# Macaron block, attention beside precomputed units: the odd chunk's scores and keys and the next values issued ahead of the q and k correction, and the router's choice cut in two

## The chip, the core and the metric

The kernel runs on one core of a Trainium2 chip. A core has a matrix engine (TensorE, PE in the profile, with PEld for its weight loads), a vector engine (VectorE, DVE), an engine for activation functions and copies (ScalarE, ACT), a general engine (GpSimd, POOL) and an engine that mostly issues transfers (SyncE, SP). Every engine works off its own queue in order and waits for the others by semaphores. Matrix products land in PSUM, a small memory of eight banks, from which VectorE or ScalarE must read them. The metric is the device time of one execution in microseconds, the median of several runs; lower is better.

## The reference, cut to what matters

```python
x = x + 0.5 * ffn(layernorm(x))      # x: 8 sequences of 1024 tokens, 512 wide, fp32
x = x + attn(layernorm(x))
x = x + 0.5 * ffn(layernorm(x))

def attn(x):                         # 16 heads of 32
    q, k, v = exp(heads(x @ Wq.T + bq)), exp(heads(x @ Wk.T + bk)), heads(x @ Wv.T + bv)
    kv, k1 = cumsum(k[..., :, None] * v[..., None, :], 1), cumsum(k, 1)
    out = einsum("zsD,zsDd->zsd", q, kv) / sum(q * k1, -1, keepdims=True)
    return unheads(out) @ Wo.T + bo

def ffn(x):                          # 32 experts; each expert chooses 8 tokens of a sequence
    probs = softmax(x @ gate_w.T + gate_b, axis=tokens)
    vals, idx = top_k(probs over tokens, 8)
    merged = sum of the 8 chosen tokens weighted by vals
    o = gelu([merged, 1] @ w1) ; o = [o, 1] @ w2
    return scatter_add(o * vals at idx)
```

The attention is linear and causal: the running sums over tokens are formed chunk by chunk, with an exact causal product inside a chunk of 128 tokens.

## The kernel before, in words

The program runs in three stages. The first FFN's router reads all eight sequences. The first FFN then streams the expert weights from HBM, and beside it `speculate` (from line 1101) already projects q, k and v of the *input* for sequences 4 to 7 and keeps the products in HBM (`ahead_d`). Attention follows (`attention`, from line 950). Last is the second FFN, again a stream of weights. Its first weights are loaded during the last sequence of attention.

Attention goes through the eight sequences b, and in each through eight chunks c of 128 tokens. Two chunks make a unit u. While a unit is attended, the next one is projected by a generator, `ahead`, which the loop advances with `next(ahead)`; each `yield` in the generator is a place where the loop goes on with something else. Up to sequence 3 the units come from `project`, which computes q, k and v in full. From sequence 4 on (in the code `rest` is true, from chunk 6 of sequence 3 to chunk 5 of sequence 7, 16 units) they come from `project_rest` (line 623). That one loads the product made beside the first FFN (tile `pre`, by `load_ahead`), scales it by the token's reciprocal deviation, and adds a correction: what the first FFN added to a token is its row of choice weights (`pm`, spread over four partition groups as `pm4`, scaled as `pmr`) times the experts' outputs already turned through Wq, Wk and Wv (`oW`, `oWv`).

Its steps are: 1. on SP, for a sequence's first unit, four loads of `pm4`, and the load of the next unit's `pre`; on POOL the bias `bo` onto `xt`, `pmr` (L651) and the two products of `pre` (L655); on PE the spread of the deviations (`ps_rs`, L641). 2. the correction of q and k: PE `ps_qk` (L667), VectorE's two additions (L676), ScalarE's eight exponentials (L679). 3. the values: PE `ps_v` (L687) and VectorE `va` (L697). 4. the running sums of the keys on VectorE (L720), and q times these sums on POOL (`qk`, L731).

For a chunk, `scores` (L777) multiplies keys with queries for all 16 heads; VectorE masks half of the result (L788), ScalarE copies the other half (L793), POOL masks that (L795). `turn_keys` (L827, copy L829) turns the keys. `attend` multiplies masked scores with values (L841) and queries with the running key-value sum (L853), divides by the denominators (L862) and adds to the running sum (L873, copy L882). `denominators` (L739, reciprocal L747) and `spread_denominators` (L758, copies L765) serve a unit. `project_out` (L891, addition L898, statistics L314 and L315) belongs to the chunk before. The generator `begun` scatters the first FFN's outputs into the next sequence (L293, L300, addition L308, statistics) over chunks 2 to 5; the generator `gate`, from `route`, runs the second FFN's router for the sequence before, a step per chunk: deviations, logits, the choice of eight tokens (`choose`, lines 404 to 428), then `ps_pmT` (L523), `ps_m` (L543) and `ps_mT` (L566).

Two things limit the order. The PSUM tiles `sp0` and `sp1` exist once: the scores, the spread denominators and the q and k correction take turns in them. Other products share three banks, `mm`. And what is written is not quite what is issued: a planner goes through the program, simulates the engines with costs of its own, and gives each engine, whenever it is free there, the ready instruction that stands first in the program. So a later instruction can run ahead of an earlier one that waits.

Of the kernel before, what the change touches and what calls it, by code (L numbers as in the profile page):

```python
# [8 lines left out]
F32 = mybir.dt.float32  # L9
AF = mybir.ActivationFunctionType  # L10
ALU = mybir.AluOpType
# [4 lines left out]
P = 128  # L16
# [4 lines left out]
def kernel(  # L21
# [52 lines left out]
    nc = tc.nc  # L74
    B, S, D = x_in.shape
# [328 lines left out]
    def choose(t, lg, rows, g, name, listed=False, el=None):  # L404


        top = t.p2.tile([P, 8], F32, tag="top", name=f"top_{name}")
        nc.vector.max(top[rows, :], lg[rows, :])
        pinned = el is not None
        sm = t.p2.tile([P, 3], F32, tag="sm", name=f"sm_{name}")  # L410
        nc.vector.tensor_scalar_mul(sm[rows, 0:1], top[rows, 0:1], -1.0)
        rest = pm[:, g, :]
        nc.vector.match_replace(rest[rows, :], top[rows, :], lg[rows, :], -1.0e30)
        if listed and not pinned:
            nc.vector.max_index(chosen_idx[rows, g, :], top[rows, :], lg[rows, :])
        el = el if pinned else lg
# [6 lines left out]
        if pinned:  # L423
            tc.keep_in_program_order(kept)
        nc.vector.reciprocal(sm[rows, 2:3], sm[rows, 1:2])
        if pinned:
            return rest, sm[rows, 2:3], top
        return rest, sm[rows, 2:3]
# [51 lines left out]
    def route(t, s, b, el=None):  # L480
# [28 lines left out]
        chosen, r, *top = choose(t, lg, rows, g, f"b{b}", True, el)  # L509
# [113 lines left out]
    def project_rest(t, s, b, u):  # L623
# [4 lines left out]
        if u == 0:  # L628

            pm4 = s["pm4"] = t.s1.tile([P, S], F32, tag="pm4", name=f"pm4_{b}")  # L630
            r0 = 32 * (b % 4)
            for j in range(4):
                nc.sync.dma_start(pm4[E * j : E * (j + 1), :], pm[r0 : r0 + E, b // 4, :])
# [25 lines left out]

        qkT = open_unit(t, s, b, u)  # L660
# [22 lines left out]

        ps = [t.mm.tile([P, D], F32, tag="mm", name=f"ps_v_{b}_{u * U + i}") for i in range(U)]
        for i in range(U):
            r = slice(E * ((b + i) % 4), E * ((b + i) % 4 + 1))
            nc.tensor.matmul(  # L687
                ps[i],
                lhsT=pmr[r, i * P : (i + 1) * P],
                rhs=s["oWv", i][r, :],  # L690
                start=True,
                stop=True,
            )
        for i in range(U):
            c = u * U + i
            va = t.a2.tile([P, D], F32, tag="va", bufs=3, name=f"va_{b}_{c}")
            nc.vector.scalar_tensor_tensor(  # L697
                va,
                pre[:, (2 * NDC + i * 2) * UT : (2 * NDC + i * 2 + 2) * UT],
                rs[:, c : c + 1],  # L700
                ps[i],
                ALU.mult,
                ALU.add,
            )
            s["va", b, c] = va
        yield
        sum_keys(t, s, b, u)
        times_keys(t, s, b, u)
        yield

# [239 lines left out]
    def attention(t, early, preload):  # L950
# [47 lines left out]
        for b in range(B):  # L998
            for c in range(NCH):
# [23 lines left out]
                if b == B - 1 and c == NCH - 2:  # L1023
# [6 lines left out]
                    )  # L1030
                    gate = route(t, s, b, el)
                if rest and c % U:
                    turn_keys(t, s, b, c)
                    next(ahead)
                    next(gate, None)
                scores(t, s, b, c)
                if c % U == 0:
                    denominators(t, s, b, c // U)
                    if (nb, nu) == (NB0, 0):
# [9 lines left out]
                        )  # L1049
                        load_ahead(t, s, nb, nu)  # L1050
# [33 lines left out]
                if not (rest and c % U):  # L1084
                    next(gate, None)
# [3 lines left out]
                if rest and c % U == 0:  # L1089
                    next(ahead)  # L1090
# [578 lines left out]
```

## Time and profile before

| | us |
|---|---|
| median of 3 runs | 2604.81 (2599.36 to 2604.91) |
| the profiled execution's own time | 2606.22 |
| its span, first to last instruction | 2604.5 |
| attention, first to last `ps_o` | 887.5 to 1940.1 |
| PE busy | 2190.8 (84%) |
| DVE, ACT, POOL busy | 862.3, 500.4, 376.6 |
| PE `ps_o` L891, 512 instructions | 258.5 |
| mean granted TensorE clock | 0.915 |

The page gives each engine's busy time. A busy PE can still run at half clock: the granted clock stands in a row of its own. Instructions are named by engine, line and tiles (what is written, an arrow, what is read), and idle time by what ended it. fp32 matrix products are issued as two instructions each, so a `scores` of 16 products appears as 32. The two FFNs are the stretches in which the DMA engines are full; attention is the stretch between, in which they are mostly idle.

### The profile page before, as it was taken

The page shows a single profiled execution, that of the slowest core. Times are in us where ns is not written, and L with a number is a line of the kernel's source. Part 1 is how long each engine was busy: PE and PEld are TensorE (multiplying, and loading weights), DVE is VectorE, ACT ScalarE, POOL GpSimd, SP SyncE. Part 2 cuts the span into 40 slices and gives each one's busy share as a digit, 9 for nine tenths or more (in the row PEclk, how much of TensorE's full clock was granted, in tenths as well). Part 3 has the DMA queues.
Part 4 walks back from the last instruction along what each step waited for, and adds up shares of the span by engine and source line. Part 5 has one row for each costly group of instructions (what it writes and reads, how often), then busy time and mean ns, then how long its engine had stood idle before and what let it go on. Part 6 is the DMA issues. An engine that isn't in the chain of part 4 may idle for free.

```text
span 2604.5 us, 41783 instructions
## 1 busy us (share of the span) xinstructions
PE 2190.8 (84%) x18679; PEld 1153.6 (44%) x18679; DVE 862.3 (33%) x1495; ACT 500.4 (19%) x965; POOL 376.6 (14%) x345
## 2 busy tenths in 40 slices
PE   8799999898986999999999989999986565555555
PEld 5354545444533666666666655555551111101111
DVE  6411111111102443444534466777750000100002
ACT  6310000000000322222223243343430000000000
POOL 0000000000000212111122145545324000000002
PEclk9999999999998999999999989989888878777788
DMA  7799999999996000010100233333159999999995
GB/s 276 305 426 427 427 427 427 426 427 428 427 429 255 1 18 1 21 50 20 52 9 19 79 110 124 106 113 109 68 210 389 425 427 428 428 428 428 428 427 239
DMA packets 95635, 668.22 MB, mean 257 GB/s; under 512 B 18254, under 2 KB 22606, under 8 KB 58592
## 3 DMA queue, kind: packets, MB, share of 16 engines
q1 hardware_dynamic: 73952, 621.71, 58.1%
q10 hardware_dynamic: 18432, 35.66, 3.5%
q0 software_dynamic: 3072, 8.19, 0.8%
q8 instruction: 146, 2.39, 0.4%
q14 instruction: 33, 0.27, 0.0%
HBM read 614.34 MB, written 48.23 MB: 254 GB/s over the span
## 4 chain that ended last, share of the span: by engine, by line
PE 50%; issue 23%; DMA 16%; DVE 5%; ACT 2%; POOL 1%; SPq 0%; POOLq 0%; ACTq 0%; DVEq 0%
DMA w<-in_w 11%; PE ps_o L891 8%; PE ps_k L603 4%; PE ps_q L603 4%; PE ps_v L811 4%; PE ps_sk L1143 3%; PE ps_sq L1143 3%; PE p_ps L1256 3%; PE h_ps L1233 3%; PE ps_n L841 2%; PE sp L777 2%; PE ps_n L853 2%; PE ps_sv L1160 2%; DMA xg<-out,chosen_idx 2%; PE ps_sc L293 1%
## 5 line engine op out<-in xcount | busy, mean ns | idle before, releaser
L1233 PE MATMUL h_ps<-w,mT 128*8 128x512 f32 x2048 | 294.4, 703 | 126.2 <-DMA w<-in_w 124.3
L1242 DVE STREAM_TRANSPOSE hs<-h_ps 128x512 f32<-128x512 f32 x64 | 45.9, 717 | 721.6 <-PE h_ps L1233 716.3
L1256 PE MATMUL p_ps<-w,pm 128*32 128x512 f32 x1024 | 168.9, 790 | 130.3 <-DMA w<-in_w 122.0
L891 PE MATMUL ps_o<-wo_sb,at 128*128 128x512 f32 x512 | 258.5, 652 | 0.2
L1233 PEld LDWEIGHTS h_ps<-w,mT 128*8 128x8 f32 x2048 | 51.2, 95 | 342.4 <-issue 208.7
L1256 PE MATMUL p_ps<-w,gl 128*32 128x512 f32 x1024 | 133.5, 654 | 38.6 <-DMA w<-in_w 38.3
L594 POOL TENSOR_TENSOR xt<-xt,bo_sb 128x512 f32<-128x512 f32 x32 | 45.8, 1447 | 763.1 <-PE ps_ocT L338 703.4
L1256 PEld LDWEIGHTS p_ps<-w,pm 128*32 128x32 f32 x1024 | 36.0, 127 | 265.7 <-issue 136.5
L891 PEld LDWEIGHTS ps_o<-wo_sb,at 128*128 128x128 f32 x512 | 102.0, 210 | 115.0 <-issue 110.0
L795 POOL TENSOR_SCALAR_AFFINE_SELECT am<-am 128x512 f32<-128x512 f32 x128 | 79.0, 642 | 398.7 <-ACT am L793 260.8
L314 DVE BATCH_NORM_STATS2 st<-xt 128x6 f32<-128x512 f32 x192 | 128.4, 684 | 5.1 <-DMA xt<-in_x 2.5
L603 PE MATMUL ps_k<-xnT,wk_sb 128*128 128x256 f32 x512 | 115.3, 383 | 10.8 <-ACT xnT L339 10.8
L1249 ACT ACTIVATE pm<-a 128x128 f32<-128x128 f32 x32 | 9.9, 309 | 586.5 <-DVE a L1244 580.5
L1143 PE MATMUL ps_sq<-xcT,wq_sb 128*128 128x256 f32 x512 | 118.7, 388 | 4.1 <-ACT xcT L241 4.1
L1143 PE MATMUL ps_sk<-xcT,wk_sb 128*128 128x256 f32 x512 | 117.4, 385 | 0.0
L1160 PE MATMUL ps_sv<-wv_sb,xcT 128*128 128x512 f32 x256 | 115.6, 599 | 0.0
L811 PE MATMUL ps_v<-wv_sb,xnT 128*128 128x512 f32 x256 | 115.1, 593 | 0.0
L603 PE MATMUL ps_q<-xnT,wq_sb 128*128 128x256 f32 x512 | 115.1, 382 | 0.0
L1143 PEld LDWEIGHTS ps_sq<-xcT,wq_sb 128*128 128x128 f32 x512 | 96.8, 193 | 35.3 <-issue 17.4
L1143 PEld LDWEIGHTS ps_sk<-xcT,wk_sb 128*128 128x128 f32 x512 | 96.8, 192 | 27.6 <-issue 15.0
L603 PEld LDWEIGHTS ps_k<-xnT,wk_sb 128*128 128x128 f32 x512 | 95.8, 190 | 28.6 <-ACT xnT L339 14.7
L777 PE MATMUL sp<-un 32*128 32x128 f32 x2048 | 104.8, 302 | 3.9 <-DVE un L676 3.8
(246 smaller groups left out, 2846.3 us busy)
## 6 DMA issues: line engine op xcount, KB each, us to landing
w<-in_w SPq DMA_DIRECT2D x256, 2048.0 KB, 29.8
xt<-in_x SPq DMA_DIRECT2D x31, 1024.0 KB, 10.8
pre<-ahead_d SPq DMA_DIRECT2D x16, 1536.0 KB, 6.5
ahead_d<-ahead_qk ACTq DMA_DIRECT2D x16, 1024.0 KB, 11.5
out<-xt SPq DMA_DIRECT2D x16, 1024.0 KB, 5.4
xs<-in_x ACTq DMA_DIRECT2D x16, 512.0 KB, 19.7
ahead_d<-ahead_v ACTq DMA_DIRECT2D x16, 512.0 KB, 11.0
pm<-pm SPq DMA_DIRECT2D x16, 128.0 KB, 2.5
```

What stands on the lines that cost most here:

```text
L314: nc.vector.bn_stats(st, xt[:, c, :])
L603: nc.tensor.matmul(ps[:, o, :], lhsT=w_sb[n][:, dc, oc * P : (oc + 1) * P], rhs=xnT[:, dc, :], start=(dc == 0), stop=(dc == NDC - 1),)
L777: nc.tensor.matmul(sp[r // 2][:, r % 2, og, :], lhsT=kT[hr, og, cols], rhs=qT[hr, og, cols], start=True, stop=True,)
L795: nc.gpsimd.affine_select(out=am[1][:, i, :, :], in_=am[1][:, i, :, :], pattern=[[0, NDC], [1, P]], compare_op=ALU.is_ge, fill=0.0, base=0 ...
L811: nc.tensor.matmul(ps, lhsT=s["xnT", b, c // U][:, dc, cols], rhs=w_sb["v"][:, dc, :], start=(dc == 0), stop=(dc == NDC - 1),)
L841: nc.tensor.matmul(ps[hr, og, :], lhsT=va[:, (og * HG + r) * HD : (og * HG + r + 1) * HD], rhs=am[r // 2][:, r % 2, og, :], start=(og == 0 ...
L853: nc.tensor.matmul(ps[hr, og, :], lhsT=kv[hr, og, :], rhs=qT[hr, og, cols], start=False, stop=True, skip_group_check=True,)
L891: nc.tensor.matmul(ps, lhsT=at[:, oc, :], rhs=w_sb["o"][:, oc, :], start=(oc == 0), stop=(oc == NDC - 1),)
L1143: nc.tensor.matmul(ps[:, o, :], lhsT=w_sb[w][:, dc, oc * P : (oc + 1) * P], rhs=xcT[:, dc, :], start=(dc == 0), stop=(dc == NDC - 1),)
L1160: nc.tensor.matmul(ps, lhsT=xcT[:, dc, i * P : (i + 1) * P], rhs=w_sb["v"][:, dc, :], start=(dc == 0), stop=(dc == NDC - 1),)
L1233: nc.tensor.matmul(h[32 * j : 32 * j + B, :], lhsT=mT[:, dc, e, :], rhs=w1h[dc // 2][:, dc % 2, j * 512 : (j + 1) * 512], start=(dc == 0), ...
L1256: nc.tensor.matmul(pp[32 * j : 32 * (j + 1), :], lhsT=gl4[e % 4][:, q, :, :].rearrange("p i b -> p (i b)"), rhs=w2h[q // (NU // 2)][:, q % ...
```

## The change

Four edits, all in attention and its router.

1. In `project_rest` the values (step 3) come ahead of the correction of q and k (step 2), and the loads of `pm4` move into a function of their own, `load_rows`, which the loop calls before the generator is made; for sequence 4 that is also ahead of the load of its first `pre` and of `oWv`.
2. In the loop, for an even chunk with `rest`, `turn_keys` and `denominators` come after step 1 of the next unit instead of, for the denominators, directly behind the scores. After `attend` of the even chunk the odd chunk's scores and keys are issued, then the next unit's values, then its correction. Before, the correction stood directly behind `attend`, and the odd chunk's keys, the values and the odd chunk's scores behind it.
3. For an odd chunk with `rest` the scores, the keys and one `next(ahead)` are gone from its start; what is left is `project_out`, the scatter step, the key sums, the router's step and `attend`. The router's step stands just ahead of `attend` in every chunk now; before, it stood ahead of the odd chunk's scores.
4. The choice becomes a generator, `choosing`: maximum, negated maximum and indices, a `yield`, and then the replacement, the exponential and the rest. The router of a sequence so takes seven steps and not six. What is left of sequence 6's router is run through before the last sequence's own begins.

```diff
     def choose(t, lg, rows, g, name, listed=False, el=None):
+        *_, made = choosing(t, lg, rows, g, name, listed, el)
+        return made
+    def choosing(t, lg, rows, g, name, listed, el=None):
...
+        in_place = el is None
+        if listed and in_place:
+            nc.vector.max_index(chosen_idx[rows, g, :], top[rows, :], lg[rows, :])
+            yield None
         nc.vector.match_replace(rest[rows, :], top[rows, :], lg[rows, :], -1.0e30)
-        if listed and not pinned:
-            nc.vector.max_index(chosen_idx[rows, g, :], top[rows, :], lg[rows, :])
...
-        chosen, r, *top = choose(t, lg, rows, g, f"b{b}", True, el)
+        for made in choosing(t, lg, rows, g, f"b{b}", True, el):
+            if made is None:
+                yield
+        chosen, r, *top = made
...
+    def load_rows(t, s, b):
+        pm4 = s["pm4"] = t.s1.tile([P, S], F32, tag="pm4", name=f"pm4_{b}")
+        r0 = 32 * (b % 4)
+        for j in range(4):
+            nc.sync.dma_start(pm4[E * j : E * (j + 1), :], pm[r0 : r0 + E, b // 4, :])
...
+                    for _ in gate:
+                        pass
                     gate = route(t, s, b, el)
-                if rest and c % U:
-                    turn_keys(t, s, b, c)
-                    next(ahead)
-                    next(gate, None)
-                scores(t, s, b, c)
+                if not (rest and c % U):
+                    scores(t, s, b, c)
                 if c % U == 0:
-                    denominators(t, s, b, c // U)
+                    if not rest:
+                        denominators(t, s, b, c // U)
...
+                        load_rows(t, s, nb)
                         load_ahead(t, s, nb, nu)
...
+                    if (nb > NB0 and nu == 0) and rest:
+                        load_rows(t, s, nb)
                     if (nb, nu) > (0, 1):
                         of = project_rest if rest else project
                         ahead = of(t, s, nb, nu) if nb < B else iter(())
                         next(ahead, None)
+                    if rest:
+                        turn_keys(t, s, b, c)
+                        denominators(t, s, b, c // U)
...
-                if not (rest and c % U):
+                if not rest:
                     turn_keys(t, s, b, c)
...
-                if not (rest and c % U):
-                    next(gate, None)
+                next(gate, None)
                 attend(t, s, b, c)
                 if rest and c % U == 0:
+                    scores(t, s, b, c + 1)
+                    turn_keys(t, s, b, c + 1)
+                    next(ahead)
                     next(ahead)
```

More of the change, by code (lines that the diff above doesn't have):

```diff
@@ L404, in choose @@
     def choose(t, lg, rows, g, name, listed=False, el=None):
+        *_, made = choosing(t, lg, rows, g, name, listed, el)
+        return made
+    def choosing(t, lg, rows, g, name, listed, el=None):
         top = t.p2.tile([P, 8], F32, tag="top", name=f"top_{name}")
         nc.vector.max(top[rows, :], lg[rows, :])
-        pinned = el is not None
         sm = t.p2.tile([P, 3], F32, tag="sm", name=f"sm_{name}")
@@ L412, in choose @@
         rest = pm[:, g, :]
+        in_place = el is None
+        if listed and in_place:
+            nc.vector.max_index(chosen_idx[rows, g, :], top[rows, :], lg[rows, :])
+            yield None
         nc.vector.match_replace(rest[rows, :], top[rows, :], lg[rows, :], -1.0e30)
-        if listed and not pinned:
-            nc.vector.max_index(chosen_idx[rows, g, :], top[rows, :], lg[rows, :])
-        el = el if pinned else lg
+        el = lg if in_place else el
         nc.scalar.activation(
@@ L422, in choose @@
         )
-        if pinned:
+        if not in_place:
             tc.keep_in_program_order(kept)
         nc.vector.reciprocal(sm[rows, 2:3], sm[rows, 1:2])
-        if pinned:
-            return rest, sm[rows, 2:3], top
-        return rest, sm[rows, 2:3]
+        yield (rest, sm[rows, 2:3]) if in_place else (rest, sm[rows, 2:3], top)
     def gather_four(t, xs, rs4, chosen, r, g):
@@ L627, in project_rest @@
         pre = s.pop(("pre", b, u))
[L628 to L633, printed above, removed]
         for i in range(U):
@@ L658, in project_rest @@
         yield
+        ps = [t.mm.tile([P, D], F32, tag="mm", name=f"ps_v_{b}_{u * U + i}") for i in range(U)]
+        for i in range(U):
+            r = slice(E * ((b + i) % 4), E * ((b + i) % 4 + 1))
+            nc.tensor.matmul(
+                ps[i],
+                lhsT=pmr[r, i * P : (i + 1) * P],
+                rhs=s["oWv", i][r, :],
+                start=True,
+                stop=True,
+            )
+        for i in range(U):
+            c = u * U + i
+            va = t.a2.tile([P, D], F32, tag="va", bufs=3, name=f"va_{b}_{c}")
+            nc.vector.scalar_tensor_tensor(
+                va,
+                pre[:, (2 * NDC + i * 2) * UT : (2 * NDC + i * 2 + 2) * UT],
+                rs[:, c : c + 1],
+                ps[i],
+                ALU.mult,
+                ALU.add,
+            )
+            s["va", b, c] = va
+        yield
         qkT = open_unit(t, s, b, u)
@@ L682, in project_rest @@
         yield
[L684 to L706, printed above, removed]
         sum_keys(t, s, b, u)
```

## The prediction, made before the changed kernel ran

> **What bounds the kernel now.** I read the page's slices first, then stretches of the attention part, then windows of 3.41 us, then one unit instruction by instruction. The edit lies in attention, where it works with units projected beside the first FFN: sixteen corrections, from 1504 us to about 1904 us. The first four lines are four stretches of about a batch each (microseconds; busy time per engine; granted TensorE clock), with 15 corrections between them; the last line is the stretch before, with the first correction.
>
> ```profile
> core 0: us, PE busy (x) PEld busy (x) DVE busy (x) ACT busy (x) POOL busy (x), PEclk, DMA share, GB/s
> 1517.00:1624.00 107.00, 99.69 (x1403) 59.19 (x1395) 78.37 (x122) 41.96 (x80) 51.34 (x42) 0.92 0.31 107
> 1624.00:1730.00 106.00, 99.35 (x1357) 59.72 (x1357) 77.23 (x120) 41.75 (x80) 50.30 (x40) 0.90 0.31 108
> 1730.00:1836.00 106.00, 98.65 (x1377) 58.05 (x1377) 78.19 (x121) 41.97 (x80) 50.31 (x40) 0.92 0.31 108
> 1836.00:1940.00 104.00, 98.76 (x1360) 59.47 (x1354) 64.75 (x98) 43.24 (x83) 32.72 (x28) 0.92 0.32 116
> ...
> 1464.00:1517.00 53.00, 45.98 (x420) 28.03 (x422) 21.07 (x32) 12.64 (x24) 16.24 (x13) 0.87 0.39 129
> ```
>
> TensorE sets the pace, but not at full speed. Its idle time in the four stretches is 7.3+6.7+7.4+5.2 = 26.6 us. The clock is 1.0 or 0.5 at any moment, so a mean of 0.92 over 107 us is 17 us at half speed; the four sum to 17+21+17+17 = 72 us, which costs 36 us. So 62.6 us is lost over 15 units, 4.2 us each. The first unit's stretch loses 7.0 us idle and 6.9 us to the clock.
>
> The next lines are single windows of the same view, chosen on the grid on which the clock changes.
>
> ```profile
> 1602.27:1605.68 3.41, 2.81 (x16) 1.65 (x13) 2.89 (x3) 2.33 (x5) 2.91 (x5) 1.00 0.00 0
> 1636.40:1639.81 3.41, 2.11 (x41) 1.52 (x37) 3.27 (x6) 2.93 (x8) 0.00 (x0) 1.00 0.02 7
> 1639.81:1643.23 3.42, 3.42 (x5) 1.46 (x5) 3.42 (x5) 3.34 (x8) 0.84 (x1) 0.50 0.86 313
> 1660.29:1663.70 3.41, 2.11 (x15) 1.10 (x11) 3.15 (x4) 1.89 (x5) 0.84 (x1) 1.00 0.00 0
> 1663.70:1667.12 3.42, 3.42 (x29) 3.42 (x32) 1.18 (x2) 1.88 (x5) 0.00 (x0) 0.50 0.54 151
> ```
>
> A window in which PE is busy 62% (2.11 of 3.41 us) is followed by one or two at half clock; one busy 82% is not. So a gap of some 1.3 us in one window costs itself and then 1.7 or 3.4 us more.
>
> Where the gap lies, a timeline of one unit shows (start, duration, engine, line, in brackets the idle time before and who ended it):
>
> ```profile
> 1716.96 1.15 PE L667 MATMUL ps_qk<-pmr,oW 32*128 32x256 f32 x16
> 1717.94 1.02 PE L687 MATMUL ps_v<-oWv,pmr 32*128 32x512 f32 x4
> 1718.19 2.36 DVE L676 TENSOR_TENSOR un<-ps_qk,pre 128x1024 f32<-128x1024 f32 x2 [0.73 <-PE ps_qk L667]
> 1719.47 0.49 PE L777 MATMUL sp<-un 32*128 32x128 f32 x4 [0.51 <-DVE un L676]
> 1720.46 1.40 DVE L697 SCALAR_TENSOR_TENSOR va<-pre,rs,ps_v 128x512 f32<-128x512 f32 x2
> 1720.60 1.16 PE L777 MATMUL sp<-un 32*128 32x128 f32 x28 [0.64 <-DVE un L676]
> 1721.69 5.40 PE L891 MATMUL ps_o<-wo_sb,at 128*128 128x512 f32 x8
> 1721.78 2.43 DVE L720 TENSOR_TENSOR_SCAN un<-ones,un 128x256 f32<-128x256 f32 x4
> 1724.38 2.36 POOL L731 TENSOR_TENSOR qk<-un 128x1024 f32<-128x1024 f32 x1 [8.05 <-DVE un L720]
> ```
>
> The odd chunk's scores (L777) need the PSUM tiles that the correction (L667) has just filled, and wait until VectorE has added them (L676). Then `ps_o` runs its first half at half clock: 5.40 us, against 3.44 us at full clock. In this unit the gaps are 0.51 and 0.64 us; in the three others of the batch it is one gap of 1.3 us. That is 1.25 us x 15 = 19 us, and every half-clock window of the four stretches follows such a gap: 19 + 36 = 55 us hang on this place.
>
> **The change part by part.** *The new order on TensorE.* From the start of an even chunk's `ps_n` (t = 0): attend 2.4 us (1714.55 to 1716.96), the odd chunk's scores 1.1, its keys 0.6, the next values 1.0, so the correction begins at 5.1. It needs the score tiles emptied: VectorE's masked product (1.20, from 3.6) ends at 4.8, ScalarE's copy (1.0) at 4.6. No wait remains. Nothing else is queued on PE behind a new wait here. Removed: 55 us.
>
> *What comes late next.* On VectorE the two `va` (1.40) now precede the two additions (2.36): these begin at 6.6, not 0.1 us after the correction. The exponentials end 4.9 us after the additions begin, as in the timeline, at 11.5. The next even chunk's scores stand on PE after the correction (to 6.1), `ps_o` (3.44) and attend (2.4): at 12.0, 0.5 us of cover. The key sums end at 11.2 (4.6 us after the additions begin), POOL's `qk` at 13.7; the denominators, moved behind the scores, the spread of rs and the keys (1.1+0.6+0.6), come at 14.3: 0.6 us of cover. The reciprocal (1.74) ends at 16.8, its reader `ps_rr` comes behind another 3.44 us of `ps_o` at 18.3. So a plain unit has no wait, with thin cover.
>
> In seven units VectorE has more: two scatter additions and two statistics (2 x 0.67 + 2 x 0.69 + 0.34 = 3.1 us a chunk, six units) or the choice. If that goes ahead of the key sums, against 1.05 us of PE work that comes with it, the denominators wait up to 3.1 - 1.05 - 0.6 = 1.4 us; if it goes behind, nothing. I take 1.0 us, nearer the full wait because VectorE is 73% busy already, and with it one window at half clock, 1.7 us. Given back: 7 x 2.7 = 19 us; bounds 0 and, as the slower rival prices it, 85.
>
> *The first unit.* PE waits 6.6 us there for `pmr` (1497.9 to 1504.5) and then runs at half clock. The four `pm4` loads now go ahead of `pre` and `oWv` on SP's queue (their issue takes 2.95 us). They can land 2.5 us after issue (page, part 6) or 9 us (as now): 1496 to 1502.5; `pre` moves from 1498.6 to 1501.5, its first product (2.3) to 1503.8. The odd chunk's scores fill 1.1 us of the wait. `ps_o`, now at 1511.1, starts at some 1505: 6 us gained; bounds 0 and 9. In later batches these loads keep their place on SP's queue, where `pre` is issued over 20 us ahead of use; its slot is now freed by the additions instead of `va`, 1 us later in the unit: nothing, and at most 1 us a unit without that cover.
>
> *The choice in two steps.* MAX8, FIND_INDEX8 and MATCH_REPLACE8 (1.2 us each) stay; the index now precedes the replacement, and what follows comes one chunk later, `ps_mT` (1.9 us on PE) in chunk 6 instead of 5. Work is moved, none added. Later: POOL and SP see one transfer, the next `xt` load behind `ps_m`, one chunk (13 us) later; the load of 10.8 us is used some 60 us on. Batches 1 to 3 have it too: there VectorE is under half busy (278 of 604 us, 860 to 1464 us), so nothing; bounds -3 and +4 us. For the last batch the leftover step is run ahead of the final router: 0, at most 1.9 us.
>
> *After attention.* The second FFN streams weights (DMA share 0.96 from 1940 us on) and starts where attention ends, so the gain passes through whole.
>
> Sum: 55 - 19 + 6 = 42 us. The profiled execution took 2606.2 us (span 2604.5), 1.4 us over the median of the runs: 2606.2 - 42 - 1.4 = 2563 us.
>
> **A rule against a row.** The rows give the half-clock windows to gaps of 1.3 us. The Trainium skill's page "TensorE: Matmul & The Clock Gate" (section "HAM oscillation — how this bites in real kernels") says that the clock drops over idle gaps longer than about 3.4 us, a whole window. By that, these gaps would not halve the clock and closing them would not give it back. The windows above contradict it: 38% idle is enough here.
>
> **The rivals.** *Nothing comes late:* 55 + 6 = 61 us, 2544. For it: every cover computed is positive. Against: 0.5 and 0.6 us of it.
>
> *Each unit gets a wait:* project_out's addition and statistics (0.69+0.69+0.18) ahead of the key sums take the 0.6 us and 1.0 more, with the half-clock window 2.7 us in all 15: 55 - 40 + 6 = 21 us, 2584.
>
> *Slower: the key sums in the written order.* They are written behind project_out and the scatter on VectorE. Held to that, they start at 11.2 (after `ps_o` at 9.5 and 1.6 us), `qk` ends at 16.1 and the denominators wait 1.8 us, with scatter 3.8; each with 1.7 to 3.4 us of half clock: 8 x 4.35 + 7 x 7.2 = 85 us against 61, so 2629. It decides from 4.1 us a unit on. For it: the written order. Against: the shown unit, where the sums (1721.78) ran ahead of the masked product written before them (1724.12), so the planner pulls ready work forward.
>
> *The half clock is not due to the gap* and stays: 19 idle + 6 - 7 = 18 us, 2587. This is where the page's rule would lead. *The change does not do it:* the planner issues much the same order: 2605.
>
> **How the numbers follow.** Chances: the forecast 0.36, nothing late 0.24, a wait in each unit 0.18, clock unrelated 0.04, no effect 0.04, slower 0.14. Faster by over 0.2% (5.2 us, about what a measurement tells from no change): 0.82; within: 0.04; slower: 0.14. The range leaves out the last two cases: up to 2600. Down to 2534, 10 us under "nothing late", since all the loss counted in the five stretches is 76 us (2528).
>
> **What would show it.** Right: no wait of the odd scores on L676's additions; the correction behind `ps_v`; four stretches near 96 us at a clock of 0.96 or more; `ps_o` at 3.4 to 3.7 us. Wrong: `ps_den` waiting for POOL `qk`, the even scores for ScalarE's exponentials, or a clock still near 0.92.

## The result, and the profile after

The changed kernel takes 2569.12 us (median of 4 runs, 2568.23 to 2570.43), the kernel before beside it 2602.09 us (2598.60 to 2604.91): a ratio of 0.9869, 95% interval 0.9849 to 0.9889. The forecast was 2563 us. So the gain is 33.0 us by the medians. The profiled execution took 2568.23 us, its span is 2566.5 us, 38.0 us less than before: one execution of each, and that of before was 4 us over the median of the kernel beside the changed one.

The edit moves the lines: scores are now L785, keys L835, values L664 and L674, the correction L692, its additions L701, key sums L728, `qk` L739, denominators L747, reciprocal L755, their spread L766, numerators L849, normalisation L870, `ps_o` L899, its addition L906. The columns of the stretches are those of before; the first line is the first unit, the others are a sequence each.

```profile
core 0: us, PE busy (x) PEld busy (x) DVE busy (x) ACT busy (x) POOL busy (x), PEclk, DMA share, GB/s
1464.00:1511.00 47.00, 46.47 (x462) 27.14 (x464) 22.91 (x35) 12.74 (x24) 16.10 (x13) 0.96 0.47 159
1511.00:1611.00 100.00, 94.18 (x1373) 56.36 (x1361) 78.48 (x120) 41.37 (x80) 49.03 (x42) 0.95 0.31 107
1611.00:1709.00 98.00, 93.04 (x1345) 55.31 (x1337) 78.87 (x120) 41.09 (x80) 50.41 (x40) 0.95 0.33 115
1709.00:1806.00 97.00, 90.49 (x1352) 53.65 (x1341) 78.20 (x120) 41.21 (x80) 50.45 (x40) 0.98 0.33 117
1806.00:1902.00 96.00, 91.27 (x1410) 55.81 (x1402) 66.50 (x102) 43.11 (x85) 35.15 (x29) 1.00 0.37 142
```

PE idles 5.8+5.0+6.5+4.7 = 22.0 us in the four stretches (26.6 before) and is at half clock for 10+10+4+0 = 24 us (72 before), which costs 12 us. So in these two executions most of what was won there came from the clock, little from idle time. The first unit's `ps_o` starts 7.0 us earlier (1504.1 against 1511.1); sequences 0 to 3 are 1.9 us shorter in it, but attention begins 2.1 us later. From there to the last `ps_o` it is 31.4 us less, and from the last `ps_o` to the end it is 664.8 us (664.4 before): attention's gain passes through whole.

The timeline of a plain unit in the new order (start, duration, engine, line):

```profile
1700.50 1.17 PE L785 MATMUL sp<-un 32*128 32x128 f32 x32
1701.51 1.03 PE L664 MATMUL ps_v<-oWv,pmr 32*128 32x512 f32 x4
1701.71 1.23 DVE L796 TENSOR_TENSOR am<-sp,mask 128x1024 f32<-128x1024 f32 x1 [0.70 <-PE sp L785]
1702.85 1.40 DVE L674 SCALAR_TENSOR_TENSOR va<-pre,rs,ps_v 128x512 f32<-128x512 f32 x2
1702.99 1.15 PE L692 MATMUL ps_qk<-pmr,oW 32*128 32x256 f32 x16 [0.45 <-DVE am L796]
1704.07 3.70 PE L899 MATMUL ps_o<-wo_sb,at 128*128 128x512 f32 x8
1704.24 2.36 DVE L701 TENSOR_TENSOR un<-ps_qk,pre 128x1024 f32<-128x1024 f32 x2
1706.51 1.84 DVE L728 TENSOR_TENSOR_SCAN un<-ones,un 128x256 f32<-128x256 f32 x3
1709.69 2.37 POOL L739 TENSOR_TENSOR qk<-un 128x1024 f32<-128x1024 f32 x1 [5.53 <-DVE un L728]
```

The odd scores wait for nobody; the correction waits 0.45 us for the masked product; `ps_o` takes 3.70 us and not 5.40, and so it does in 12 of the 16 units, where before every one took 4.67 us or more. What idle time is left, the groups of PE instructions from 1516 to 1900 us show (after the bar: busy us, mean ns, idle us before them and who ended it):

```profile
L664 PE MATMUL ps_v<-oWv,pmr 32*128 32x512 f32 x60 | 20.0, 630 | 1.8 <-DVE at L870 1.8
L692 PE MATMUL ps_qk<-pmr,oW 32*128 32x256 f32 x240 | 18.9, 419 | 1.4 <-DVE am L796 1.4
L835 PE MATMUL ps_kt<-ident,un 128*128 128x128 f32 x108 | 17.1, 281 | 4.2 <-DVE xt L308 4.2
L766 PE MATMUL ps_rr<-rd,hrep 32*128 32x256 f32 x128 | 11.4, 427 | 4.6 <-DVE rd L755 4.6
L550 PE MATMUL ps_m<-xt,pmT 128*32 128x512 f32 x64 | 10.0, 758 | 4.1 <-DVE xt L906 4.1
L747 PE MATMUL ps_den<-qk,hsum 128*32 128x256 f32 x120 | 9.8, 395 | 1.5 <-DVE mv L315 1.0
```

Nearly all of it is VectorE: ScalarE ends 1.7 us beside these lines, and no wait is put down to `qk`. How VectorE comes to be late, a chunk 2 shows:

```profile
1732.90 1.22 DVE L413 MAX8 top_b<-lg 32x8 f32<-32x1024 f32 x1 [1.46 <-ACT lg L400]
1734.15 1.29 DVE L308 SCALAR_TENSOR_TENSOR xt<-ps_sc,xt 128x512 f32<-128x512 f32 x2
1734.90 0.66 PE L835 MATMUL ps_kt<-ident,un 128*128 128x128 f32 x4 [1.41 <-DVE xt L308]
...
1737.17 1.22 DVE L419 FIND_INDEX8 chosen_idx<-top_b,lg 32x8 uint32<-32x1024 f32 x1
...
1739.57 1.75 DVE L755 RECIPROCAL rd<-ps_den 128x256 f32<-128x256 f32 x1
...
1741.37 0.71 PE L766 MATMUL ps_rr<-rd,hrep 32*128 32x256 f32 x8 [1.51 <-DVE rd L755]
```

MAX8 stands at the head of VectorE's queue and waits 1.46 us there for ScalarE's logits, with the scatter addition behind it; that one holds an `mm` bank which the key turn needs (1.41 us). FIND_INDEX8 and the masked product behind it then stand ahead of the reciprocal, and the spread waits 1.51 us.

### The profile page after: what moved, and what is told of

The parts are those of the page before. It is cut to its first block, busy times and chain, and to the rows that moved or that the text cites. A ratio compares the mean times of both kernels' runs of the same rounds, so it can differ in the third digit from the quotient of the medians.

```text
span 2566.5 us, 41820 instructions
## 1 busy us (share of the span) xinstructions
PE 2160.2 (84%) x18679; PEld 1137.4 (44%) x18679; DVE 867.7 (34%) x1495; ACT 497.9 (19%) x965; POOL 377.1 (15%) x345
## 4 chain that ended last, share of the span: by engine, by line
PE 47%; issue 23%; DMA 16%; DVE 7%; ACT 1%; POOL 1%; POOLq 0%; ACTq 0%; DVEq 0%; SPq 0%
DMA w<-in_w 12%; PE ps_o L899 7%; PE ps_k L610 4%; PE ps_q L610 4%; PE ps_v L819 4%; PE ps_sq L1160 3%; PE ps_sk L1160 3%; PE h_ps L1250 3%; PE p_ps L1273 3%; PE sp L785 2%; PE ps_n L849 2%; DMA xg<-out,chosen_idx 2%; PE ps_sv L1177 2%; PE ps_n L861 2%; DVE st L314 1%
## 5 line engine op out<-in xcount | busy, mean ns | idle before, releaser
L1250 PE MATMUL h_ps<-w,mT 128*8 128x512 f32 x2048 | 281.5, 683 | 118.8 <-DMA w<-in_w 118.2
L1273 PE MATMUL p_ps<-w,pm 128*32 128x512 f32 x1024 | 179.5, 837 | 138.5 <-DMA w<-in_w 133.5
L899 PE MATMUL ps_o<-wo_sb,at 128*128 128x512 f32 x512 | 240.6, 614 | 1.1 <-ACT rsb L650 1.1
L899 PEld LDWEIGHTS ps_o<-wo_sb,at 128*128 128x128 f32 x512 | 95.3, 196 | 111.4 <-issue 105.0
L610 PEld LDWEIGHTS ps_q<-xnT,wq_sb 128*128 128x128 f32 x512 | 96.0, 190 | 15.5 <-ACT un L619 0.8
```

The lines of the kernel that those rows point to most:

```text
L610: nc.tensor.matmul(ps[:, o, :], lhsT=w_sb[n][:, dc, oc * P : (oc + 1) * P], rhs=xnT[:, dc, :], start=(dc == 0), stop=(dc == NDC - 1),)
L899: nc.tensor.matmul(ps, lhsT=at[:, oc, :], rhs=w_sb["o"][:, oc, :], start=(oc == 0), stop=(oc == NDC - 1),)
L1250: nc.tensor.matmul(h[32 * j : 32 * j + B, :], lhsT=mT[:, dc, e, :], rhs=w1h[dc // 2][:, dc % 2, j * 512 : (j + 1) * 512], start=(dc == 0), ...
L1273: nc.tensor.matmul(pp[32 * j : 32 * (j + 1), :], lhsT=gl4[e % 4][:, q, :, :].rearrange("p i b -> p (i b)"), rhs=w2h[q // (NU // 2)][:, q % ...
```

## The experiments

Each kernel ran beside the kernel before on the same chip; ratios are to that. The table also gives, from one profiled execution each, the stage from `ps_o` of sequence 3's chunk 5 to `ps_o` of sequence 7's chunk 7, PE's idle time in it (its busy intervals joined) and half of the time at half clock.

| kernel | median us | ratio, 95% interval | stage us | idle | lost to half clock |
|---|---|---|---|---|---|
| before | 2602 to 2608 | 1 | 445.8 | 33.4 | 42.5 |
| changed | 2569.12 | 0.9869 (0.9849-0.9889) | 407.2 | 22.6 | 13.6 |
| changed, again | 2568.85 | 0.9866 (0.9848-0.9884) | 408.0 | 21.4 | 15.3 |
| order alone | 2582.70 | 0.9922 (0.9905-0.9939) | 419.6 | 33.5 | 18.7 |
| choice alone | 2597.17 | 0.9950 (0.9931-0.9969) | 433.1 | 38.6 | 18.7 |
| all but the order | 2597.93 | 0.9961 (0.9945-0.9977) | 435.6 | 41.5 | 13.6 |
| all but the choice | 2574.04 | 0.9860 (0.9843-0.9877) | 415.0 | 25.8 | 20.4 |
| all but the late denominators | 2576.32 | 0.9877 (0.9860-0.9895) | 418.6 | 31.3 | 17.0 |
| all but the early rows | 2573.86 | 0.9878 (0.9857-0.9900) | 414.4 | 24.5 | 20.4 |
| changed, MAX8 pinned | 2577.38 | 0.9872 (0.9855-0.9890) | 408.3 | 21.0 | 20.4 |
| changed, one to a chunk | 2563.12 | 0.9837 (0.9818-0.9856) | 403.8 | 22.0 | 15.3 |
| changed, `ps_pmT` over 128 rows | 2564.34 | 0.9845 (0.9828-0.9863) | 405.2 | 23.4 | 10.2 |
| both joined, mended | 2550.88 | 0.9781 (0.9764-0.9797) | 391.7 | 15.8 | 6.8 |

Two cautions on the last column. It is an upper bound: with the choice alone idle time and half clock together fall by 18.6 us and the stage by 12.7, with all but the order by 20.8 and 10.2, so part of the half clock of before cost nothing. And it is one execution of each. The granted clock of every execution is on record; one minus it, times the span, over the whole program, averages 223 us in 30 executions of before (211 to 235), 202 in eight of the changed kernel (195 to 211), 202 with the choice alone (197 to 205), 212 with the order alone (206 to 222), 196 with all but the order (189 to 203), 190 with `ps_pmT` over 128 rows (187 to 195) and 178 with both joined (176 to 181). So the clock gives the change some 21 us of its 33, and the order alone wins about half as much clock as its profiled execution shows.

**The order, taken back** ("all but the order"). In the changed kernel `ps_qk` goes ahead of the values in the generator again, and the loop issues:

```diff
-                    scores(t, s, b, c + 1)
-                    turn_keys(t, s, b, c + 1)
-                    next(ahead)
-                    next(ahead)
+                    next(ahead)
+                    turn_keys(t, s, b, c + 1)
+                    next(ahead)
+                    scores(t, s, b, c + 1)
```

> The changed kernel with the order of before at this one place: correction of q and k, odd keys, next values, odd scores. The choice in two steps, the late denominators and the early rows of the first unit stay. Theory of the prediction: the odd scores again wait for VectorE's additions, 1.3 us in each of 15 units, and about one window of half clock per unit follows: idle of TensorE up by 15 to 20 us, and in all 2595 to 2610. Rival: the gain came from the denominators moved behind the keys or from the choice: then it stays within 2569 to 2580.

Measured 0.9961: 0.9% (24 us) of the gain hangs on the order. But the half clock did not come back: 13.6 us as in the changed kernel. What came back is idle time, and in two places (lines as in the changed kernel, additions at L677):

```profile
L849 PE MATMUL ps_n<-am,va 128*32 128x128 f32 x958 | 44.8, 293 | 15.1 <-POOL am L803 14.9 <-DVE am L796 0.2
L785 PE MATMUL sp<-un 32*128 32x128 f32 x928 | 44.6, 286 | 11.1 <-DVE un L677 11.1
L766 PE MATMUL ps_rr<-rd,hrep 32*128 32x256 f32 x120 | 11.2, 445 | 9.7 <-DVE rd L755 9.7
```

The scores wait for the additions as the theory has it. The larger wait, 14.9 us, is one that neither the theory nor its rival had: the numerators wait for POOL's masking of the late scores.

**The choice alone.** The kernel before with part 4 of the change and nothing else: `choosing`, its call in `route`, and the leftover step ahead of the last router.

> Before, with the choice in two steps alone (the index and the replacement a chunk apart, the leftover step run ahead of the last router). The prediction costed this at nothing, with bounds of -3 and +4 us: expected 2602, between 2599 and 2606, since no work is added and the steps move one chunk in a stream in which VectorE is under three quarters busy. Rival: the split is what relieves VectorE in chunks 2 to 5 of the later batches, and so part of the whole change's 33 us is its: then 2585 to 2596.

Measured 0.9950, 10 us by the medians: outside the bounds of -3 and +4 that the prediction gave it, and within the rival's 6 to 17 us. But VectorE's relief is not how. First the groups before, then those of this kernel (scores L784, numerators L848):

```profile
L777 PE MATMUL sp<-un 32*128 32x128 f32 x896 | 50.1, 315 | 3.5 <-DVE un L676 3.5
L841 PE MATMUL ps_n<-am,va 128*32 128x128 f32 x928 | 36.4, 276 | 1.5 <-POOL am L795 1.5
L523 PE MATMUL ps_pmT<-diag,pm 32*128 32x32 f32 x64 | 9.7, 306 | 5.2 <-DVE va L697 5.2
L566 PE MATMUL ps_mT<-isum,m 128*128 128x32 f32 x24 | 5.1, 371 | 3.9 <-DVE va L697 3.9
L388 PE MATMUL ps_rs<-rsT,pick 8*128 8x128 f32 x16 | 2.8, 296 | 5.2 <-DVE va L697 5.2
```

```profile
L784 PE MATMUL sp<-un 32*128 32x128 f32 x960 | 48.8, 298 | 6.0 <-DVE un L683 6.0
L848 PE MATMUL ps_n<-am,va 128*32 128x128 f32 x960 | 41.8, 280 | 11.5 <-POOL am L802 11.3 <-DVE am L795 0.2
```

The half-clock loss fell from 42.5 to 18.7 us (over all executions the mean granted clock gives some 21 us less) although the wait for the additions and `va` is all there: 6.0 us at the scores and 5.2 us each at `ps_m` and `ps_rs`, which come first in other units, 16.4 us; in before it is 3.5+5.2+3.9+5.2 = 17.8 us in the same way. A window of this kernel with such a gap, and the next one:

```profile
1636.43:1639.84 3.41, 2.18 (x36) 1.67 (x37) 3.27 (x6) 3.19 (x8) 0.00 (x0) 1.00 0.25 48
1639.84:1643.25 3.41, 3.17 (x11) 1.09 (x9) 3.41 (x5) 2.93 (x6) 1.67 (x1) 1.00 0.91 360
```

64% busy, and the clock stays at 1.00, against the prediction's reading that 62% trips and 82% does not. Where `ps_o` runs at full speed its 1.7 us are not won: POOL's masking is not done earlier, and the numerators now wait for it, 11.3 us against 1.5. In the kernel before, the half clock had hidden that wait. Why the split moves the half clock is only argued: in before the windows that trip are 27.3 us, eight windows, or 23.9 us, seven, apart (from 1530.59, 1557.89, 1585.20, 1612.51 to 1636.40), so each gap met the grid at the same place, with little work beside it; with the steps of the choice a chunk later that is over. The 36 us that the prediction hung on the half clock could not be had in full by curing the clock alone: more than half of it goes here, and 10 us come. The new order takes both, since the odd scores end 2.4 us ahead of `ps_o` (1701.67 to 1704.07 in the unit above) and not just as it starts (1721.76 and 1721.69 in the unit of before, where modelled ends overlap a little), and POOL masks them meanwhile.

**The order alone.** The changed kernel with the three edits that follow below together (choice, denominators and rows taken back), so that only the odd scores, keys and values ahead of the correction are left.

> The new order at the correction alone: odd scores, odd keys and next values ahead of the correction of q and k. The choice is in one step, the denominators are directly behind the even scores and the first sequence's rows are loaded last, all as in before. Theory from the runs so far: of the 33 to 38 us of the whole change, undoing the choice costs 5, undoing the place of the denominators 7 and undoing the rows 5; the order alone is left with about 18 to 22 us: 2583 to 2588. Rival: the parts are not additive, and without the late denominators the order gains little, because POOL's product then holds up every unit: 2592 to 2600.

Measured 2582.70 us, 0.9922: 21 us, as the theory had it. Order alone (0.78%) and choice alone (0.50%) add up to 1.28% of the 1.31 to 1.34% of the whole, each with an interval of about 0.2% to either side.

The wait at the scores is gone, but PE's idle time is not: 33.5 us in the stage, as before. It has moved: to waits for VectorE like those of the changed kernel (4.4, 4.3 and 4.1 us), to `ps_o` once (4.3 us) and to the denominators (this kernel's groups of PE instructions):

```profile
L746 PE MATMUL ps_den<-qk,hsum 128*32 128x256 f32 x120 | 9.6, 391 | 5.1 <-POOL qk L738 5.1
```

So in the profiled execution the order alone wins by the clock, and the idle time comes down only where the other parts stand beside it.

**The choice taken back.** The changed kernel without the step:

```diff
             nc.vector.max_index(chosen_idx[rows, g, :], top[rows, :], lg[rows, :])
-            yield None
```

> The changed kernel with the choice in one step again (no chunk between the index and the replacement). Theory: TensorE's waits at chunk 2 come from MAX8 standing at the head of VectorE's queue, and MAX8 stands there with or without the split; 2569 within 5 us, with the same 1.3 us ahead of the key turn in each of three batches. Rival: in the new order VectorE has no room for the 3.6 us of the choice in one chunk, and the split is what keeps the reciprocal of the denominators in time: the spread of the denominators then waits up to 2.4 us more in each of four batches, with a window at half clock (1.7 us) each, 16 us: 2585.

The waits at chunk 2 are the same (4.2 us ahead of the key turn), which fits the theory; 2574.04 us lies at the edge of the theory's 5 us and does not reach the rival's 2585. The price of the choice in the new order is not settled: the ratio (0.9860) differs from the changed kernel's by less than the intervals, and towards the faster side, while the stage of the one profiled execution is 7 to 8 us longer. More can't be said.

**The denominators, ahead of the keys again.** In the loop:

```diff
                 if c % U == 0:
-                    if not rest:
-                        denominators(t, s, b, c // U)
+                    denominators(t, s, b, c // U)
...
                     if rest:
                         turn_keys(t, s, b, c)
-                        denominators(t, s, b, c // U)
```

> The changed kernel with the denominators directly behind the even scores again, as in before, ahead of the spread of rs and the keys. Theory of the prediction: moving them was what keeps them from waiting for POOL's product; in the changed kernel that product ends 0.7, 1.2, 1.2, 1.2, 0.7 and 0.5 us after the even scores in six of the sixteen units and before their end in the others, so the denominators wait 5.5 us in all, with one to three half-clock windows (1.7 us each) more: 2574 to 2580, where the changed kernel takes 2569. Rival: the denominators' wait only takes the place of the waits for the reciprocal behind them (1.0 to 1.5 us in three or four units), and the time stays within 2 us.

By the ratios (0.9877 against 0.9866) too little to tell. By the medians it is 7 us, but the kernel before was 4 us slower beside it too; by the stage 11 us, but that execution was the longest of its four (2572.44 to 2580.76). The wait that was forecast is in this kernel's groups of PE instructions:

```profile
L747 PE MATMUL ps_den<-qk,hsum 128*32 128x256 f32 x120 | 9.6, 391 | 5.3 <-POOL qk L739 5.3
L899 PE MATMUL ps_o<-wo_sb,at 128*128 128x512 f32 x242 | 115.9, 623 | 4.5 <-ACT rsb L650 4.3
```

5.3 us of the 5.5 expected; the changed kernel's line has no such wait. The second line was not expected: at one place in the last sequence `ps_o` waits 4.3 us for ScalarE's copy of the spread deviations, where the changed kernel waits 1.1. Order alone, the other kernel with the early denominators, shows the same 4.3; how they cause it was not followed. The cover that the prediction worked out (0.6 us in a plain unit) is real and in places thinner: in the changed kernel's second execution `qk` ends 0.06 us before the denominators start in three of the sixteen units.

**The rows, loaded last again.** For sequence 4:

```diff
-                        load_rows(t, s, nb)
                         load_ahead(t, s, nb, nu)
...
                         nc.sync.dma_start(oWv[:E], s["oWv", 0][3 * E :])
+                        load_rows(t, s, nb)
```

> The changed kernel with the four loads of rows for the first projected sequence behind its other loads on SP's queue again, as in before; nothing else. Theory of the prediction: the first unit loses about 5 of the 7 us that it gained, the rest of it (about 1 us) being the odd scores that now fill the wait: 2573 to 2575 where the changed kernel takes 2569. Rival: the gain of the first unit comes from the odd scores and from the window at full clock, not from the loads: within 1.5 us of the changed kernel.

2573.86 us, 5.0 more than the changed kernel beside it, as the theory had it (the interval of the ratio, 0.9857 to 0.9900, does not exclude less). In this kernel's timeline the values of the first unit wait for `pmr` again:

```profile
1500.10 1.29 PE L664 MATMUL ps_v<-oWv,pmr 32*128 32x512 f32 x2 [4.03 <-POOL pmr L652]
```

**Once more, and the clock's grid.** The changed kernel without an edit.

> The changed kernel once more, unchanged, beside the three kernels sent with it, and to see whether the half-clock windows fall at the same places in another execution. Theory: the 3.41 us grid of the clock stands anywhere against the program (the profiles so far have it at 0.42, 0.68, 0.42, 0.87, 0.32 and 0.91 of a window), so that the same instructions with the same waits give other half-clock windows; the sum over the four later sequences stays near 12 us, the time within 3 us of 0.987 of before. Rival: the grid is locked to the program and the windows come at the same instructions.

The time repeats (0.9866). In this execution the clock's grid stands at 0.55 of a window from the first instruction (0.68 in the first profile), and the windows that trip are other ones than in the first profile: of the three chunk 2 gaps of 1.3 to 1.4 us, the first one trips and the others do not; in the first profile it was the second. So a single half-clock window is no property of the kernel; the sum (13.6 and 15.3 us) nearly is. The Trainium skill says the same ("TensorE: Matmul & The Clock Gate", "What's actually happening": the window is free-running, and its place against the kernel differs from run to run); these two traces agree.

**What the clock goes by.** In all thirteen traces I took the windows of the grid from 900 to 1900 us that ran at full clock, 3650 of them, and gave each an array share: the time that matmuls stream (0.84 ns a column from the start of each, from `ps_o`'s 3.44 us for 8 times 512), each weighted by rows times columns of the array in use over 128 times 128, over 3.41 us. Of 3469 windows with a share of 0.40 or more none is followed by half clock; of 90 between 0.34 and 0.40, 44; of 91 below, 64. PE's busy time does not sort them: of 142 windows busy 55 to 75%, 61 trip, and 12 that are busy 99% or more trip as well. All twelve hold `ps_pmT`, a product on 32 rows that streams 32 columns to a matmul. To test the share, that product is taken over all 128 rows, the rest of its right-hand side being zero:

```diff
+        nc.gpsimd.memset(diag, 0.0)
...
-                lhsT=chosen[rows, c * P : (c + 1) * P],
-                rhs=diag[rows, :],
+                lhsT=chosen[:, c * P : (c + 1) * P],
+                rhs=diag,
```

> The changed kernel with the transposed choice multiplied over all 128 rows (the other rows of the right-hand side are zero) instead of 32: as many instructions, as many columns, the same result, and TensorE's order the same. A window of 3.41 us with the transposed choice in it was 100 per cent busy in the profile of the changed kernel and was still followed by half clock; its streaming weighted by rows times columns of the array was 0.34 (8 other trips 0.13 to 0.34, no trip at 0.38 or more). Theory: the clock goes by that weighted share, so these windows rise to about 0.45 and no window that holds the transposed choice whole trips any more; time 0 to 5 us less. Rival: the clock goes by idle time or by the number of short matmuls; then fully busy windows with it trip as before, and the time stays.

Windows with this product, and the next one each; the changed kernel (its second execution), then with 128 rows:

```profile
1664.17:1667.58 3.41, 3.41 (x64) 2.93 (x59) 1.55 (x4) 1.07 (x2) 3.41 (x2) 1.00 0.80 195
1667.58:1671.00 3.42, 3.42 (x64) 2.71 (x64) 0.42 (x1) 0.37 (x1) 0.46 (x1) 0.50 0.98 304
```

```profile
1668.49:1671.90 3.41, 3.41 (x60) 2.90 (x56) 1.14 (x4) 1.24 (x3) 3.06 (x3) 1.00 0.91 264
1671.90:1675.31 3.41, 3.41 (x118) 2.68 (x106) 1.22 (x2) 0.89 (x3) 0.00 (x0) 1.00 0.74 207
```

Fully busy both times. In sequences 4 to 7 of this execution with 32 rows all three windows that hold the whole product trip (shares 0.34 to 0.35), with 128 rows none of four (0.38 to 0.47). Over all profiles ten of thirteen fully busy windows with the whole product on 32 rows and a share of at most 0.36 trip. No instruction of PE changed its place in the order. The times, 2562.96 to 2564.95 us, lie below all of the changed kernel's in the same set (2567.04 to 2570.23), though the ratios' intervals overlap. So for these windows it is the rows in use that decide, and not idle time; that columns count in the same way is not tested. The Trainium skill ("TensorE: Matmul & The Clock Gate", section "HAM oscillation — how this bites in real kernels") has the clock drop over idle gaps above 3.4 us; here it drops after windows without any gap.

The share is not the whole rule. Between 0.34 and 0.40 it is not sharp, and 27 windows below 0.34 stay at full clock. 25 of these hold twenty or more matmuls of the numerators, which use only 32 columns of the array each: with so many of them 9 of 34 windows below 0.34 trip, with fewer 55 of 57. So the share gives the numerators too little; by what weight they count is open. Some of these windows are the choice-alone kernel's (1619.4, 1643.3 and 1769.6 us: busy 61, 56 and 71%, shares 0.26 to 0.30, no trip): there PE idles among the numerators.

**What was given back: VectorE's order.** MAX8 is held to its written place.

```diff
-        nc.vector.max(top[rows, :], lg[rows, :])
+        tc.keep_in_program_order(nc.vector.max(top[rows, :], lg[rows, :]))
```

> The changed kernel with MAX8 of the choice held at its written place on VectorE (behind the addition and statistics of the output projection in chunk 2), instead of at the head of the queue where it waits 1.5 us for the logits. No instruction is added or left out. Theory: what was given back (about 14 us of idle and half clock) hangs on VectorE's order: the 4.2 us ahead of the key turns and 3 of the 4.6 us ahead of the spread of the denominators go, with two or three half-clock windows (1.7 us each): 2557 to 2563. Rival: VectorE's total work in chunks 2 to 5 is the bound, and the wait only moves, to the output projection that needs the normalised values behind MAX8, FIND_INDEX8 and MATCH_REPLACE8 (3.6 us): 2566 to 2580.

The waits at the key turn and the spread are gone (no gap above 0.4 us there in any sequence), so their cause is shown. The time is not better (0.9872): MAX8, FIND_INDEX8 and MATCH_REPLACE8 now stand together ahead of the masked product that frees the correction's tiles, 2.1 us in each of the four sequences (this kernel's groups of PE instructions):

```profile
L692 PE MATMUL ps_qk<-pmr,oW 32*128 32x256 f32 x240 | 21.3, 465 | 9.6 <-DVE am L796 9.6
```

The rival was right that the wait moves, and wrong on where to. Besides, sequences 1 to 3, which the pin also met, took 6 us longer. Next, one of the three to a chunk, a further `yield` behind MAX8 and all three pinned, for the routers run from sequence 4 on (the edit of the joined version below, with "b6" too and FIND_INDEX8 held as well):

> The changed kernel with MAX8, FIND_INDEX8 and MATCH_REPLACE8 of the last four routers before the final one held at their written places, one to a chunk (chunks 2, 3 and 4). Pinning MAX8 alone took the waits ahead of the key turn and the spread of the denominators away (1.4 and 1.5 us), and put one of 2.06 us ahead of the correction in each sequence, because the three stood together, 3.6 us, ahead of the masked product of chunk 3. Theory: one to a chunk, 1.2 us, fits; neither wait is there, idle time of the four later sequences falls from 22 to 14 or 16 us, and the time to 2556 to 2564. Rival: VectorE has no room of 1.2 us in any of these chunks, and each of the three makes a wait of its own: idle again 20 us or more, 2567 to 2578.

0.9837, in the theory's range by the time, but not by the mechanism: idle time stayed at 22.0 us. FIND_INDEX8, pinned in chunk 3, goes ahead of the addition to `xt` that frees a bank, and the numerators wait up to 2.86 us (this kernel's group; the addition is L910):

```profile
L853 PE MATMUL ps_n<-am,va 128*32 128x128 f32 x1024 | 36.4, 285 | 8.3 <-DVE xt L910 8.3
```

**Both joined.** MAX8 and FIND_INDEX8 in chunk 2, MATCH_REPLACE8 in chunk 4, for three routers; the last sequence left as it was; `ps_pmT` over 128 rows.

```diff
+        late = listed and el is None and name in ("b3", "b4", "b5")
+        held = tc.keep_in_program_order if late else id
-        nc.vector.max(top[rows, :], lg[rows, :])
+        held(nc.vector.max(top[rows, :], lg[rows, :]))
...
         if listed and in_place:
+            if late:
+                yield None
             nc.vector.max_index(chosen_idx[rows, g, :], top[rows, :], lg[rows, :])
             yield None
-        nc.vector.match_replace(rest[rows, :], top[rows, :], lg[rows, :], -1.0e30)
+        held(nc.vector.match_replace(rest[rows, :], top[rows, :], lg[rows, :], -1.0e30))
```

> Two parts joined: the transposed choice over 128 rows (alone: 2564), and the choice of three of the four later routers held to MAX8 and FIND_INDEX8 in chunk 2 (2.4 us) and MATCH_REPLACE8 in chunk 4; the last sequence is as in the changed kernel (with one to each chunk it took 2.7 to 4.2 us longer there). Theory: the 2.86 us ahead of the numerators in chunk 3, which came from FIND_INDEX8 standing ahead of the addition that frees a PSUM bank, goes; in its place the correction waits some 0.9 us (2.06 us with 3.6 us of work ahead); with the bank's wait gone the window there holds its share and stays at full clock: 2548 to 2557. Rival: VectorE's work is the bound whatever the order, idle stays at 20 us or more, and only the two known gains add: 2558 to 2564.

2550.88 us (2547.74 to 2552.21), 0.9781 (0.9764 to 0.9797): better than both kernels. Its four stretches:

```profile
1509.00:1603.00 94.00, 90.48 (x1371) 55.07 (x1365) 77.75 (x122) 41.40 (x80) 51.43 (x44) 0.98 0.36 123
1603.00:1697.00 94.00, 90.77 (x1353) 55.86 (x1349) 76.62 (x120) 41.14 (x80) 50.22 (x42) 0.96 0.35 120
1697.00:1791.00 94.00, 90.50 (x1373) 54.53 (x1365) 77.61 (x123) 41.40 (x80) 51.17 (x42) 0.98 0.35 124
1791.00:1882.00 91.00, 86.39 (x1361) 53.14 (x1358) 64.50 (x97) 42.63 (x83) 34.10 (x29) 1.00 0.33 124
```

91 to 94 us a sequence where the changed kernel takes 96 to 100, idle 3.5+3.2+3.5+4.6 = 14.8 us, with VectorE busy nearly as long (296 us against 302). The correction waits 0.46 us, not the 0.9 expected, and the numerators' 2.86 us have become 0.99. So VectorE's total work was not the bound; the order of three instructions was. Three windows here that hold most or half of `ps_pmT` over 128 rows still trip, but PE idles for about 1 us in each (busy 66 to 71%, shares 0.19 to 0.22).

## Why the prediction was right, and where not

The forecast of 2563 us was 6 us low, with 42 us of gain against 33.0 by the medians and 38.0 between the two profiled spans. The direction and the place were right; that the size came so near is in part luck, for two errors cancel. Point by point:

- *Removed, 55 us (19 idle, 36 half clock).* The place was right: nothing waits for the additions now. The 19 us of idle time are about as counted (17.8 at these waits), but with the order alone they came back at other waits. The 36 us were mis-read. The step that failed is "every half-clock window of the four stretches follows such a gap", taken for "hangs on this place": with the choice in two steps alone the gap stays, more than half of the half clock goes, and the time falls by 10 us only, with POOL's masking of the late scores behind it (11.3 us). The order by itself is worth 21 us, first unit included, and 24 us beside the other parts.
- *Given back, 19 us in seven units, from the denominators.* The forecast left 62.6 - 55 + 19 = 27 us of idle time and half clock in the four stretches; 22.0 + 12 = 34 us are left. VectorE was rightly named. The mechanism was not: the denominators do not wait for `qk`. The `mm` banks are held, and the reciprocal is late, because the choice and the scatter stand ahead of them on VectorE. The denominators' own thin cover held because they were moved: ahead of the keys they wait 5.3 us.
- *The choice, 0 (bounds -3 and +4).* Wrong in the old order, where it gains 10 us; in the new one open between nothing and 7. No wait in the trace of before shows it. That the sum came out is luck here: this gain made up for the too large one of the order.
- *First unit, 6 us.* Its `ps_o` starts at 1504.1 us, 7.0 earlier; from `ps_o` of chunk 5 to that of chunk 7 it takes 26.6 us with the rows last, with them first 22.8 and 20.5 (the latter with `ps_o` at full clock), so some 4 to 6 of it is theirs.
- *Sequences 0 to 3, within -3 and +4:* 1.9 us less. *After attention, nothing:* 0.4 us.
- *Signs.* No wait on the additions, the correction behind `ps_v`, `ps_o` at 3.70 us in 12 of 16 units: seen. "Four stretches near 96 us at 0.96 or more": 100, 98, 97 and 96 at 0.95, 0.95, 0.98 and 1.00, the forecast's on the last two only. The sign against it, `ps_den` waiting for `qk`, appeared only where the denominators were moved back (5.1 and 5.3 us; 0.6 or less elsewhere).
- *The rule against the row.* That gaps far under 3.4 us precede half clock was right. "82% busy stays, 62% trips" was not a rule: the array shares of those windows were 0.66 and 0.27 to 0.33, and a window busy 64% at 0.47 stays.
- *Rivals.* That the half clock is not due to the gap (2587, chance 0.04) was nearer to what happened than its chance: the gap alone does not make it, though the new order does lessen it (42.5 to 18.7 us with the order alone in one execution, some 12 us over all). Nothing late (2544) missed what VectorE holds up; a wait of the denominators in every unit (2584) was seen in none of these kernels. Key sums in the written order (2629) did not come: they ran ahead of the output projection's addition (1706.51 against 1708.28 in the unit shown).

## What to carry to other kernels

A stall that a lower clock follows need not be worth both: ask what else would wait if the clock stayed up, for the half clock can hide another engine's lateness as an ordinary matmul can. When a planner pulls an instruction ahead because nothing ready stands before it, look at what queues behind its wait; moving three instructions of 1.2 us within one engine's queue, and widening one product, was worth some 18 us by the medians (22 by the ratios). And read the clock from how many rows of the array the work fills too, not only from how long PE is busy.

## What the hardware showed that was not expected

- A fully busy 3.41 us window can be followed by half clock: fully busy windows that hold the whole of `ps_pmT` on 32 rows, at an array share of 0.33 to 0.36, were in ten cases of thirteen, those with it on 128 rows (0.38 to 0.47) in none of four.
- The grid of these windows stands anywhere from 0.13 to 0.99 of a window over the profiles, and differed between two executions of one kernel (0.68 and 0.55), so one profile's half-clock windows must not be assigned to instructions one by one; only their number nearly repeats (8 and 9).
